# Expert work moved beside the recurrent layer, parts of the row work and of the gathers moved ahead, and one PSUM bank fewer for the decays

## The chip, the cores and the metric

The kernel runs on one core of a Trainium2 chip. That core has five engines that run side by side: PE (TensorE, matrix products), DVE (VectorE), ACT (ScalarE, functions from tables), POOL (GpSimd) and SP (SyncE, which only issues transfers here). Each engine takes its instructions in the order in which the program gave them to it. They wait for each other by semaphores. The metric is the time of one execution in microseconds (us), and the number given for a kernel is the median of its runs.

## The reference, cut to what matters

The input is x with 4 batches of 32 x 96 tokens of 256 features. Two layers follow each other.

```python
# layer 0: two Mamba blocks, along the 96 positions ("t"), then along the 32 variables ("d")
h = exp(dt * A) * h + dt * B * u          # a recurrence over the tokens, 16 states per channel
y = (h * C).sum(states) ; ...
# layer 1, attention: every pair of the 3072 tokens of a batch, 32 units
e = (tanh(q[:, :, None, :] + k[:, None, :, :] + bh) @ Wa) + ba ; t = t + softmax(e) @ t_norm
# layer 1, graph and experts, on rows that are normalized again
h = x @ W_gat ; a_src, a_dst = per-head sums
e = leaky_relu(a_src[src] + a_dst[dst])   # 1048576 random edges, softmax by destination
scores -> layer norm -> top 2 of 4 experts -> softmax gates g
out = out + g[..., ei] * (gelu(x @ W1[ei] + b1[ei]) @ W2[ei] + b2[ei])    # all 4 experts, all rows
```

The indices of the edges reach past the 12288 rows: an edge with a destination outside is dropped, one with a source outside counts for the last row, and the others are sorted into 432 columns of 128 edges and gathered. Expert work is independent of the graph until the gates weigh it.

## The kernel before, in words

The work is laid out in three stretches.

**Layer 0 (class `Layer0`)** works in 64 blocks of 384 tokens. A block has 48 slots. In two of three slots there is a pair of decays on ACT (line 371, `dA<-dt`: an exponential per state, into PSUM), the matching pair of scans on DVE (line 388, `h<-dA,dB`) and a product on POOL (line 395). The decays go round robin through `DA_BUFS` = 3 PSUM banks, so that ACT may be up to three decays ahead of the scans. The front of the next block (projections, convolution, softplus) runs in the same slots; its softplus uses two tiles, `ua` and `ub`.

**Attention (class `Attention`)** of a batch has 768 columns. In each column ACT takes a tanh over 128 x 3072 (line 790, `th<-krep,qsel`), and PE multiplies it by the weights of the units (line 766, `pe<-th`) two columns later. Every eighth column a unit ends: a maximum on DVE, an exponential on ACT (line 841, `pr`), transposes (line 848) and values (line 857) on PE. Every fourth unit ends a tile of 128 rows, for which POOL writes four small tiles (line 907, `sf`) that PE waits for. Keys of the next batch (`keys`) and the normalization of finished rows (`after`, one run of 24 tiles for a batch) are taken a step at a time from the list `side`, in columns with nothing else to do.

`whole` weaves the two: one column of attention for one slot of layer 0, written out by hand in a fixed order for PE, ACT, DVE and POOL. Layer 0 of the first batch runs alone. Attention of batches 0 to 2 then runs beside layer 0 of the later batches; these are the shared stretches. When layer 0 has ended, attention of the last batch runs beside the sorting of the edges (class `Edges`, on DVE, with one-hot products on PE) and beside `Experts.early`. `early` works on *units*: a unit is one expert on one block of 512 rows, and there are 24 blocks and 4 experts, 96 units. `early` is given budgets of PE time per column, covers the blocks of the first two batches expert by expert, and stores results in DRAM (`kept`). When attention ends, `after` of the last batch runs, four steps of `early` to each of its steps.

**The tail (`tail`)** does the units that are left and the graph. POOL gathers for each of the 432 edge columns one row of `tab_s` (by source) and one of `tab_d` (by destination), both on line 1253. 36 parts of 12 columns are scored on DVE and ACT and placed by PE (line 1294, `pa`), in four quarters; after a quarter its gates are computed, and kept results of its blocks are read back, weighed and added (line 1503). The order is a list of slots: three slots to a unit, a gather every `PART`/2 slots.

Of the kernel before, what the change touches and what calls it, by code (L numbers as in the profile page):

```python
# [26 lines left out]
P = 128  # L27
# [12 lines left out]
DA_BUFS = 3  # L40
# [4 lines left out]
KQ = TOK // NQT  # L45
LAG = 2
# [15 lines left out]
G0, PART = 4, 8  # L62
# [11 lines left out]
class Layer0:  # L74
# [8 lines left out]
    def __init__(self, ctx, tc, ident, a, x1):  # L83
# [5 lines left out]
        self.dram = pool("l0d", 1, space=bass.MemoryType.DRAM)  # L89
        ps_a = pool("l0a", 1, space=PSUM)  # L90
        self.dA = [ps_a.tile([P, 512], F32, tag=f"dA{i}", name=f"dA{i}") for i in range(DA_BUFS)]
        self.turn = 0
# [67 lines left out]
    def scale_states(self, t):  # L160
        nc = self.nc
        nc.scalar.activation(t["A"], t["A"], AF.Exp)
        nc.vector.tensor_scalar(t["A"], t["A"], -1.0, None, ALU.mult)
        nc.vector.tensor_scalar(t["D"], t["D"], 0.5, None, ALU.mult)

    def front(self, blk, lead):
# [94 lines left out]
        def _():  # L261
# [8 lines left out]
            v["ua"] = wk.tile([P, EC, T], F32, tag="ua", name="ua")  # L270
            v["ub"] = wk.tile([P, EC, T], F32, tag="ub", name="ub")
# [265 lines left out]
    def run(self):  # L537
# [34 lines left out]
        for n, blk in enumerate(blocks):  # L572
# [16 lines left out]
            for slot in range(48):  # L589
# [13 lines left out]
                if slot == 42 and then:  # L603
# [4 lines left out]
                    if fresh:  # L608
                        self.wf = self.weights(blocks[n + 2]["way"], FRONT)
                        self.scale_front(self.wf)  # L610
                yield (old["b"] if old and slot == 11 and (old["way"], old["i"]) == ("d", NBLK - 1)
# [11 lines left out]
class Attention:  # L623
# [4 lines left out]
    def __init__(self, ctx, tc, ident, a, x1, x2, xn2T, tab_s, tab_a):  # L628
# [31 lines left out]
        self.extra, self.entry = 0.0, 0  # L660
# [11 lines left out]
    def inverse_roots(self, mv):  # L672

        rs = self.rows.tile([P, NT], F32, tag="lrs", name="lrs")
        self.nc.scalar.activation(rs, mv[:, :, 1], AF.Sqrt, bias=self.eps)
        self.nc.vector.reciprocal(rs, rs)
# [21 lines left out]
    def keys(self, b):  # L698
# [13 lines left out]
        krep = self.rows.tile([P, TOK], F32, tag="krep", name="krep")  # L712
        qsel = self.rows.tile([P, TOK // R_ATT], F32, tag="qsel", name="qsel")
# [40 lines left out]
    def units(self, side):  # L754
# [24 lines left out]
        while i < B * PER + LAG or todo:  # L779
            b, col = self.entry, _ = divmod(i, PER)  # L780
# [36 lines left out]
            if b and col == LAG + 10:  # L817
                side.append(self.after(b - 1))
# [3 lines left out]
        side.append(self.after(B - 1))  # L822
# [104 lines left out]
    def after(self, b):  # L927

        nc, mv = self.nc, self.state[b]["mv2"]
        N = NT // CT  # L930
        x2 = self.x2[b * TOK:(b + 1) * TOK, :]
        x = self.tiles_of(x2, 0)
        rs = self.inverse_roots(mv)
        yield
        for j in range(N):
# [27 lines left out]
            nc.sync.dma_start(self.tab_a[:, n0:n0 + CT, :], db)  # L963
# [3 lines left out]
class Edges:  # L967
# [6 lines left out]
    def __init__(self, ctx, tc, a):  # L974
# [8 lines left out]
        self.nc.sync.dma_start(self.lanes, a["lanes"])  # L983

# [51 lines left out]
    def sort(self):  # L1036
# [4 lines left out]
        with ExitStack() as ctx:  # L1041
# [60 lines left out]
            for of, rows in ((s3, self.si), (x3, self.di)):  # L1102
# [3 lines left out]
                v.tensor_scalar(hi, d, 7, None, ALU.logical_shift_right)  # L1106
                v.tensor_tensor(flat(rows), lo, hi, ALU.add)
# [58 lines left out]
class Graph:  # L1166
# [4 lines left out]
    def __init__(self, ctx, tc, a, ed, tab_s, tab_a, tab_d, gates):  # L1171
        self.nc, self.ed = tc.nc, ed
        self.tab_s, self.tab_a, self.tab_d, self.gates = tab_s, tab_a, tab_d, gates
# [28 lines left out]
    def tables(self):  # L1202
# [3 lines left out]
        adst = new("adst", [P, NH, 2 * HEADS])  # L1206
        nc.sync.dma_start(hall, self.tab_s)
        nc.sync.dma_start(adst[:, :, 0:HEADS], self.tab_a)
# [5 lines left out]
        top, topa = new("top", [P, HEADS]), new("topa", [P, HEADS])  # L1214
        nc.vector.tensor_reduce(top, hall[:, :, 0:HEADS].rearrange("p n h -> p h n"), AX.X, ALU.max)
# [5 lines left out]
        nc.sync.dma_start(self.tab_d, adst)  # L1221
# [23 lines left out]
    def gather(self, j):  # L1245
        nc, ed = self.nc, self.ed
        gs = self.wk.tile([P, GP, ROW], F32, tag="gs", name="gs", bufs=4)
        gd = self.wk.tile([P, GP, 2 * HEADS], F32, tag="gd", name="gd", bufs=4)
        q, c0 = divmod(j * GP, CQ)
        rows = lambda t: t.rearrange("p n f -> (p n) f")  # L1250
        for u in range(GP):
            for to, table, idx in ((gs, self.tab_s, ed.si), (gd, self.tab_d, ed.di)):
                nc.gpsimd.indirect_dma_start(  # L1253
                    out=to[:, u, :], out_offset=None, in_=rows(table),
                    in_offset=bass.IndirectOffsetOnAxis(ap=idx[:, q, c0 + u:c0 + u + 1], axis=0))
        self.got[j] = gs, gd

    def scores(self, j):
        nc = self.nc
        gs, gd = self.got.pop(j)  # L1260
        e = self.wk.tile([P, GP, HEADS], F32, tag="e", name="e")
        v = self.wk.tile([P, GP, ROW], F32, tag="v", name="v")
# [602 lines left out]
```

## Time and profile before

| what | value |
|---|---|
| median of 3 runs | 15634.05 us (15623.67 to 15639.06) |
| profiled execution | 15643.13 us, its span 15641.4 us |
| busy, share of the span | PE 75%, DVE 71%, ACT 77%, POOL 58% |
| layer 0 of the first batch, alone | 0 to about 2560 us |
| shared stretches with the changes of batch | about 2560 to 11150 us |
| attention of the last batch, edges, early units | to 13988 us |
| rows of the last batch, early units | to 14198 us |
| tail | 14198 to 15641 us |

Times inside the profile are counted from the span's start. A row of the groups gives line, engine, operation, the tiles written and read, their shapes and a count; behind the first bar the busy time and the mean of one in ns; behind the second the idle time of the engine just before them and what ended it. PE records an fp32 product twice. A row of the stages gives the length, then for PE, weight loads, DVE, ACT and POOL busy time and count, then the granted clock of PE, the share of the DMA engines and GB/s.

### The profile page before, as it was taken

The numbers are of one execution on the slowest core, as the hardware profiler recorded it, in microseconds if no ns is written. First come the engines' busy times: TensorE is split into PE (matmuls) and PEld (weight loads), VectorE is DVE, ScalarE is ACT, GpSimd is POOL, SyncE is SP. The second block draws the span as 40 slices with busy tenths as digits, with TensorE's granted clock in tenths as the row PEclk, the third lists the DMA queues.
The fourth block names the chain that finished last, engine by engine and source line by source line (L and its number), as shares of the span: only waits on it lengthen the run. The fifth ranks groups of instructions, "written<-read, shape, count | busy, mean of one in ns | idle before, by whom it ended". The sixth has DMA issues, their size and how long they took to land.

```text
span 15641.4 us, 222408 instructions
## 1 busy us (share of the span) xinstructions
PE 11808.2 (75%) x85872; PEld 5087.3 (33%) x85872; DVE 11045.8 (71%) x15303; ACT 12053.9 (77%) x9331; POOL 9052.0 (58%) x6586
## 2 busy tenths in 40 slices
PE   5666665777777767777777777777778788889988
PEld 2222222222222232222223322222233344446545
DVE  7888888777777787777778876777677733323455
ACT  3443335999999979999998899999979899971211
POOL 4555557777777767777777675777500000004774
PEclk8888886888888888888888888888889999999999
DMA  5666665444445444444444443454310000013223
GB/s 188 203 202 203 199 198 160 149 145 151 148 146 150 154 151 145 145 148 147 148 149 150 151 147 115 143 152 151 121 47 28 17 8 8 21 36 82 43 62 101
DMA packets 1168144, 1959.71 MB, mean 125 GB/s; under 512 B 408545, under 2 KB 612961, under 8 KB 1164897
## 3 DMA queue, kind: packets, MB, share of 16 engines
q1 hardware_dynamic: 1139424, 1939.16, 39.8%
q0 software_dynamic: 27648, 6.25, 0.8%
q8 instruction: 675, 11.06, 0.3%
q14 instruction: 397, 3.24, 0.1%
HBM read 1841.73 MB, written 103.28 MB: 124 GB/s over the span
## 4 chain that ended last, share of the span: by engine, by line
ACT 37%; PE 20%; DVE 17%; POOL 12%; issue 10%; DMA 4%; SPq 0%; DVEq 0%; POOLq 0%; ACTq 0%
ACT th L790 27%; PE pe L766 9%; DVE h L388 6%; ACT dA L371 6%; POOL h L395 4%; POOL gs L1253 3%; POOL gd L1253 3%; PE pv L857 2%; DVE dB L379 2%; ACT pr L841 2%; DMA bB<-bc 2%; PE ptw L848 1%; PE po L1432 1%; POOL ub L305 1%; PE ph L1424 1%
## 5 line engine op out<-in xcount | busy, mean ns | idle before, releaser
L790 ACT ACTIVATE th<-krep,qsel 128x3072 f32<-128x3072 f32 x3072 | 8666.3, 2848 | 327.1 <-PE pe L766 309.7
L766 PE MATMUL pe<-th,wa_blk 128*32 128x384 f32 x49152 | 5118.1, 547 | 1893.1 <-ACT pr L841 1536.3
L395 POOL TENSOR_TENSOR h<-h,bC 128x768 f32<-128x768 f32 x2048 | 3785.0, 1848 | 2561.5 <-DVE h L388 2310.8
L388 DVE TENSOR_TENSOR_SCAN h<-dA,dB 128x384 f32<-128x384 f32 x4096 | 3683.3, 940 | 787.4 <-ACT dA L371 601.8
L766 PEld LDWEIGHTS pe<-th,wa_blk 128*32 128x32 f32 x49152 | 1472.2, 118 | 4581.0 <-issue 1989.1
L379 DVE TENSOR_TENSOR dB<-bB,dtu 128x768 f32<-128x768 f32 x2048 | 1946.2, 950 | 131.7 <-DMA bB<-bc 87.5
L371 ACT ACTIVATE dA<-dt,t_A 128x380 f32<-128x380 f32 x2048 | 1122.1, 570 | 879.6 <-DVE h L388 873.9
L907 POOL TENSOR_SCALAR sf<-sel,f 128x32 f32<-128x32 f32 x384 | 152.5, 421 | 2639.2 <-ACT f L903 2522.0
L371 ACT ACTIVATE dA<-dt,d_A 128x372 f32<-128x372 f32 x2048 | 1097.8, 562 | 557.3 <-DVE h L388 551.8
L414 PE MATMUL py<-h,ident 128*128 128x384 f32 x2176 | 1000.6, 592 | 680.0 <-POOL h L395 678.7
L402 POOL TENSOR_TENSOR h<-h 128x768 f32<-128x768 f32 x752 | 1422.9, 1892 | 46.6
L850 DVE COPY pT<-ptw 128x512 f32<-128x512 f32 (+1 forms) x768 | 425.7, 554 | 1149.6 <-PE ptw L848 1148.4
L857 PE MATMUL pv<-xn,pT 128*32 128x257 f32 x18432 | 1090.6, 384 | 84.3 <-DVE pT L850 83.5
L414 PEld LDWEIGHTS py<-h,ident 128*128 128x128 f32 x2176 | 438.1, 219 | 1243.8 <-POOL h L395 1016.1
L403 POOL TENSOR_TENSOR h<-h 128x384 f32<-128x384 f32 x752 | 803.0, 1068 | 59.0
L404 POOL TENSOR_TENSOR y<-y,h 128x384 f32<-128x384 f32 x752 | 773.7, 1029 | 59.0
L857 PEld LDWEIGHTS pv<-xn,pT 128*32 128x32 f32 x18432 | 584.4, 111 | 638.3 <-DVE pT L850 169.5
L1500 ACT ACTIVATE h<-ph,b 128x512 f32<-128x512 f32 x248 | 165.2, 686 | 702.8 <-PE ph L1424 702.4
L1253 POOL DMA_INDIRECT gs<-tab_s,si x432 | 501.6, 1161 | 131.7 <-issue 127.1
L1253 POOL DMA_INDIRECT gd<-tab_d,di x432 | 487.3, 1128 | 134.7 <-issue 130.1
L309 DVE SCALAR_TENSOR_TENSOR ua<-ub,ua 128x384 f32<-128x384 f32 x256 | 429.2, 1677 | 190.5 <-POOL ub L305 186.3
L1432 PE MATMUL po<-w,h 128*128 128x256 f32 x1984 | 471.9, 393 | 54.7 <-DVE o L1493 38.4
(280 smaller groups left out, 14868.4 us busy)
## 6 DMA issues: line engine op xcount, KB each, us to landing
bB<-bc SPq DMA_DIRECT2D x2048, 384.0 KB
bC<-bc SPq DMA_DIRECT2D x2048, 384.0 KB
x<-x SPq DMA_DIRECT2D x144, 256.0 KB
kept<-ko SPq DMA_DIRECT2D x68, 512.0 KB
all<-kept SPq DMA_DIRECT2D x17, 2048.0 KB
xt<-xn2T SPq DMA_DIRECT2D x59, 512.0 KB
x<-x SPq DMA_DIRECT2D x192, 128.0 KB
xs<-in_xT SPq DMA_DIRECT2D x16, 768.0 KB
```

The costliest lines, as they stand in the source:

```text
L371: nc.scalar.activation(inner(dA[:, :T]), inner(blk["dt"][:, e, :]), AF.Exp, scale=blk["w"]["A"][:, e, i + s:i + s + 1])
L379: nc.vector.tensor_tensor(dB, blk["bB"].pop(j), z["dtu"].unsqueeze(1).to_broadcast([P, SB, T]), ALU.mult)
L388: nc.vector.tensor_tensor_scan(h[:, s, :], z.pop(("dA", e, i + s))[:, :T], z["dB"][:, s, :], 0.0, ALU.mult, ALU.add)
L395: nc.gpsimd.tensor_tensor(h, h, blk["bC"].pop(j), ALU.mult)
L402: nc.gpsimd.tensor_tensor(h0, h0, h1, ALU.add)
L403: nc.gpsimd.tensor_tensor(h0[:, 0, :], h0[:, 0, :], h0[:, 1, :], ALU.add)
L404: nc.gpsimd.tensor_tensor(y[e], y[e], h0[:, 0, :], ALU.add)
L414: nc.tensor.matmul(z["py"], self.ident, h[:, s, :], start=(i == 0), stop=(i == DS - 1))
L766: nc.tensor.matmul(pe[q * QU:(q + 1) * QU, j, :KQ // 2], self.wa[:, k, :], th[:, c0:c0 + KQ // 2], start=(k == 0), stop=(k == NK - 1))
L790: nc.scalar.activation(th, s["krep"], AF.Tanh, bias=s["qsel"][:, col:col + 1])
L857: nc.tensor.matmul(pv[q * QU:(q + 1) * QU, :C + 1], pT[:, i, q * QU:(q + 1) * QU], s["xn"][:, q * NK + i, :], start=(i == 0), stop=(i == N ...
L1253: nc.gpsimd.indirect_dma_start(out=to[:, u, :], out_offset=None, in_=rows(table), in_offset=bass.IndirectOffsetOnAxis(ap=idx[:, q, c0 + u: ...
```

## The change

It has several parts.

- **`Beside`**: 25 jobs in the slots of the shared stretches. A job is three half units (256 rows each) of one expert. In a block's 48 slots it has six pairs of products (slots 0 to 12), one gelu over 128 x 3072 on ACT (slot 14), and six output products (slots 15 to 29). Each product goes into one new PSUM bank, which DVE drains a slot later. Weights, rows and bias lie in the tiles that the keys of the next batch will take.
- `DA_BUFS` falls from 3 to 2: its bank is the one that `Beside` uses. `ua` and `ub` become one tile, `uab`, which takes turns with the hidden units of a job (`eh`).
- `after` of a batch runs in four parts, as its tiles end, each with its own inverse roots.
- Of 432 gathers by destination, 324 (first three batches) are issued in attention of the last batch, three to a column, once the edges are sorted; they read `tab_a`, now a table for each batch. `tab_d` goes; what it held is computed for each part on DVE. The gathers of a part are put ten slots ahead of its scores, and the first ahead of the tables.
- `early` covers three batches, without the units that `Beside` has done.

Counted in the two programs' instruction lists, units fall as follows: beside layer 0, from 0 to 37 (and a half); in `early`, from 34 to 22; in the tail, from 62 to 37.

```diff
-DA_BUFS = 3
+DA_BUFS = 2
+AFTER = (0, 8), (8, 16), (16, 22), (22, 24)
...
-G0, PART = 4, 8
+G0, PART = 10, 6
...
-            v["ua"] = wk.tile([P, EC, T], F32, tag="ua", name="ua")
-            v["ub"] = wk.tile([P, EC, T], F32, tag="ub", name="ub")
+            uab = self.wide("uab")
+            for i, k in enumerate(("ua", "ub")):
+                v[k] = uab[:, i * EC * T:(i + 1) * EC * T].rearrange("p (e t) -> p e t", e=EC)
...
+                if self.beside:
+                    self.beside(slot, then is None or then["way"] != blk["way"] == "d")
                 yield (old["b"] if old and slot == 11 and (old["way"], old["i"]) == ("d", NBLK - 1)
...
-        krep = self.rows.tile([P, TOK], F32, tag="krep", name="krep")
-        qsel = self.rows.tile([P, TOK // R_ATT], F32, tag="qsel", name="qsel")
+        krep, qsel = self.krep[b % 2], self.qsel[b % 2]
...
             if b and col == LAG + 10:
-                side.append(self.after(b - 1))
+                side.append(self.after(b - 1, *AFTER[-1]))
+            side += [self.after(b, t0, t1) for t0, t1 in AFTER[:-1]
+                     if b < B and col == t1 * P // R_ATT + LAG + 10]
...
+    def gather(self, q, c):
+        if (q, c) not in self.have:
+            self.have.add((q, c))
+            self.nc.gpsimd.indirect_dma_start(
+                out=self.gd[:, q, c, :], out_offset=None,
+                in_=self.tab_a[q].rearrange("p n f -> (p n) f"),
+                in_offset=bass.IndirectOffsetOnAxis(ap=self.di[:, q, c:c + 1], axis=0))
...
-        nc.sync.dma_start(self.tab_d, adst)
...
-            for to, table, idx in ((gs, self.tab_s, ed.si), (gd, self.tab_d, ed.di)):
-                nc.gpsimd.indirect_dma_start(
...
+            nc.gpsimd.indirect_dma_start(
+                out=gs[:, u, :], out_offset=None, in_=rows,
+                in_offset=bass.IndirectOffsetOnAxis(ap=ed.si[:, q, c0 + u:c0 + u + 1], axis=0))
+            ed.gather(q, c0 + u)
...
-        nc.vector.tensor_tensor(e, e, gd[:, :, HEADS:], ALU.subtract)
+        nc.vector.tensor_tensor(sh, gd, self.topa.unsqueeze(1).to_broadcast([P, GP, HEADS]), ALU.add)
+        self.leaky(sh)
+        nc.vector.tensor_tensor(e, e, sh, ALU.subtract)
...
+class Beside:
+    PRODUCTS = {0: (0, 0), 3: (0, 1), 5: (1, 0), 8: (1, 1), 10: (2, 0), 12: (2, 1)}
+    GELU = 14
+    OUTPUTS = {15: (0, 0), 17: (0, 1), 20: (1, 0), 23: (1, 1), 26: (2, 0), 29: (2, 1)}
...
+        if (not self.jobs or last or att.asked > att.entry + 1 or att.col < 40
+                or self.jobs[0][0] >= min(att.normed, att.entry)):
+            return
+        b, e, j = self.job = self.jobs.pop(0)
+        place = att.krep[(att.entry + 1) % 2]
...
+            if slot - 1 in self.PRODUCTS:
+                k, f2 = self.PRODUCTS[slot - 1]
+                for f in (2 * f2, 2 * f2 + 1):
+                    nc.vector.tensor_scalar(self.h[:, k, f, :], self.ps[:, f % 2, :],
+                                            self.b1[:, e, f:f + 1], None, ALU.add)
+            if slot - 1 in self.OUTPUTS:
...
+                nc.vector.tensor_tensor(o, self.ps[:, 0, :], self.b2, ALU.add)
+                i, n = divmod(self.first + k, 2)
+                nc.sync.dma_start(self.kept_block(i)[:, 2 * n + q, e, :], o)
+            if slot in self.PRODUCTS:
+                k, f2 = self.PRODUCTS[slot]
+                self.ps = self.bank()
+                for f in (2 * f2, 2 * f2 + 1):
+                    for c in range(KC):
+                        nc.tensor.matmul(self.ps[:, f % 2, :], self.w1[:, c, f * P:(f + 1) * P],
+                                         self.xt[:, c, :], start=(c == 0), stop=(c == KC - 1))
...
+            if slot == self.GELU:
+                h = self.h.rearrange("p k f m -> p (k f m)")
+                nc.scalar.activation(h, h, AF.Gelu)
...
-            t = 3 * G0 + PART * m // 2
-            at(t, lambda j=j: gr.gather(j))
-            t += 10
+            t = G0 + PART * m // 2
+            if m < 1:
+                gr.gather(j)
+            else:
+                at(max(0, t - 10), lambda j=j: gr.gather(j))
             at(t, lambda j=j: gr.scores(j))
...
-                    if units is None and att.entry == B - 1:
+                    if units is None and att.entry == B - 1 == att.normed:
...
-                            [(i, e) for e in range(NEXP) for i in range(NBLK_X // 2)], a, place)
+                            [(i, e) for i in range(NBLK_X - NBLK_X // B) for e in range(NEXP)
+                             if (i, e) not in ex.done], a, att.krep[B % 2])
...
+                    for _ in range(3 if columns else 0):
+                        ed.gather(*columns.pop(0))
```

## The prediction

> **What bounds the kernel now.** I read first the page's slices, then the stages, then the groups of the bounding engine, then the order of time where two stages meet. The slices of ACT and POOL:
>
> ```profile
> ACT  3443335999999979999998899999979899971211
> POOL 4555557777777767777777675777500000004774
> ```
>
> ACT is full from slice 7 to slice 35, but for the two changes of batch; POOL is idle for eight slices and busy again at the end. The stages (length; then PE, weight loads, DVE, ACT, POOL) say it in numbers:
>
> ```profile
> 2560.00:5400.00 2840.00, 2107.10 (x18009) 787.81 (x18008) 2212.24 (x2860) 2754.95 (x2079) 2205.30 (x1573) 0.86 0.48 149
> 6000.00:8300.00 2300.00, 1708.61 (x14680) 627.48 (x14676) 1783.25 (x2248) 2233.65 (x1686) 1792.68 (x1279) 0.87 0.47 147
> 12500.00:13990.00 1490.00, 1307.73 (x13684) 602.23 (x13688) 473.75 (x877) 1445.44 (x588) 20.41 (x60) 0.94 0.04 13
> 14230.00:15485.00 1255.00, 1133.12 (x3414) 671.13 (x3413) 580.36 (x963) 254.71 (x336) 987.44 (x863) 0.95 0.28 65
> ```
>
> In both shared stretches and in the attention of the last batch ACT is busy 97%: what is added to ACT there lengthens the kernel, what is added to PE, DVE and POOL may fit. In the tail POOL has 987 us of 1255, and between its gathers 0.30 us of issue each:
>
> ```profile
> L790 ACT ACTIVATE th<-krep,qsel 128x3072 f32<-128x3072 f32 x3072 | 8666.3, 2848 | 327.1 <-PE pe L766 309.7 <-DVE krep L733 11.4
> L1253 POOL DMA_INDIRECT gs<-tab_s,si x432 | 501.6, 1161 | 131.7 <-issue 127.1 <-DMA gs<-tab_s,si 4.6
> L1253 POOL DMA_INDIRECT gd<-tab_d,di x432 | 487.3, 1128 | 134.7 <-issue 130.1 <-DMA tab_d<-adst 3.3 <-DMA gs<-tab_s,si 1.2
> ```
>
> So a gather costs 1.145 + 0.30 = 1.45 us there, 864 of them 1253 us, which is the stage. The tail is POOL's until 15485; PE needs less, since one unit, 16 records of `ph` and twice 16 of `po`, takes 13.77 us once gathers are over (15543.11 to 15556.88):
>
> ```profile
> 15543.11 3.62 PE L1432 MATMUL po<-w,h 128*128 128x256 f32 x16
> 15546.56 1.88 PE L1424 MATMUL ph<-xt,w 128*128 128x512 f32 x4
> 15548.28 3.62 PE L1432 MATMUL po<-w,h 128*128 128x256 f32 x16
> 15551.73 5.31 PE L1424 MATMUL ph<-xt,w 128*128 128x512 f32 x12
> 15556.88 3.62 PE L1432 MATMUL po<-w,h 128*128 128x256 f32 x16
> ```
>
> 62 units at 13.77 and 108 placings at 3.38 us make 1219 us.
>
> **Gain: from the end of attention (13988) to the end.** Before this takes 15641 - 13988 = 1653 us: 242 until gathers start at 14230 (12 units of `early` and twelve pairs of tiles of `after` lie there), 36 parts x 34.8 = 1253, then 158. After, by the instruction lists: one pair of tiles and one pair of units are left, and the first part's gathers stand ahead of the tables. POOL needs the last write of `tab_s`: the pair of tiles takes about 36 us (before, its first ran from 14001 to 14027, and here its rows must first be written and read back). Parts 0 to 8 still gather both tables: 9 x 24 x 1.45 = 313. The other 27 gather 12 x 1.45 = 17.4 us each, less than PE's share of a part, one unit and three placings: 13.77 + 10.14 = 23.9. PE sets these: 27 x 23.9 = 645, and 6% for waits on `rh`, 39 (PE was busy 86 to 90% there while it waited for POOL; I take a third of that). PE trails POOL by 13. The last gates take 22 (15516 to 15541 before, with other work between). Then six blocks of kept results: 16 additions x 0.485 = 7.8 us, about 10 with their reads, 60, and 10 for the last store. Sum 36 + 313 + 13 + 645 + 39 + 22 + 70 = 1138. **Gain 515**; 440 if additions wait for their 2 MB reads, 560 if POOL's quieter price (0.94 + 0.30) holds.
>
> **Cost 1: ACT in the shared stretches.** 25 gelus of 3072 are new. No such row exists; the nearest are gelu of 2048 (1.91 us) and tanh of 3072 (2.848), so 2.85 x 25 = 71. Each needs other tables than the exponentials. The lists show 235 table loads ahead of the tail after against 164 before: 50 by gelus, 24 by 12 more inverse roots, three fewer elsewhere. What one costs:
>
> ```profile
> 13886.55 1.28 ACT L1467 ACT_TABLE_LOAD   x1
> 13887.85 3.71 ACT L1467 ACTIVATE h<-h 128x2048 f32<-128x2048 f32 x2
> ```
>
> 1.30 from its start to the next start, and it begins 0.02 after the tanh ends. The Trainium skill, "ScalarE: Activation LUTs", "What ACT_TABLE_LOAD costs", adds a drain of 1.38 us to a switch, 2.66 in all. By the rule 71 loads cost 189 us, by the row 92. I see no drain in this row (before the load the tanh has its usual 2.84) and take 92. With 3 for the roots **166 us**, all on the bound; 263 by the rule.
>
> **Cost 2: two banks for decays.** With three, decay k waits for scan k-3; with two, for scan k-2. I set the recorded start of every decay in the trace against the recorded end of scan k-2. In layer 0 alone decays come later, but no scan would: ACT is under 40% busy there and finishes a decay while DVE is at the next scan and product. In the shared stretches, if everything else stayed put, new waits sum to 114 us (69, 38 and 7); if a delay once taken is never made up but moves all, 12. Most of the 114 would fall into gaps ACT has anyway. **40**, and 10 at the changes of batch (16 and 148 by the same ways; ACT is not the bound there).
>
> **Cost 3: PE and DVE of the jobs.** A product of 512 rows and half the columns costs PE 0.45 us (16 records 3.62), so a slot with a piece gets 1.8 us more. A column lasts about 3.6 us (one tanh and four thirds of a decay) and holds 2.66 of PE (74%): 4.5 in 12 of 32 slots, 2.66 in the rest. ACT may run two columns ahead of PE (three `th` tiles, two columns' lag), which covers 0.9 us and the 0.9 of the next piece; where a piece meets a unit's values (2.8 us) it doesn't. About one such meeting a job at 1.2 us: **30**, between 0 and 120. Draining costs DVE 7.6 us a job (18 x 0.42), under its 78% load; if that cover were gone it would be 190. Each job adds to SP three row loads behind PE's products, six stores behind DVE, and at times weights; the reads of `bB` and `bC` stand behind them, two ahead of need. I take nothing, for SP's waits are on work of the same slot.
>
> **Cost 4: gathers ahead.** The list puts all 324 gathers into attention's last four tiles, 96, 96, 96 and 36 between the `sf` groups. POOL takes them in order, ahead of `sf`:
>
> ```profile
> 13712.56 1.36 POOL L907 TENSOR_SCALAR sf<-sel,f 128x32 f32<-128x32 f32 x4 [92.58 <-ACT f L903]
> 13814.26 1.36 POOL L907 TENSOR_SCALAR sf<-sel,f 128x32 f32<-128x32 f32 x4 [100.35 <-ACT f L903]
> 13917.55 1.36 POOL L907 TENSOR_SCALAR sf<-sel,f 128x32 f32<-128x32 f32 x4 [101.93 <-ACT f L903]
> ```
>
> 96 gathers at 1.25 are 120 us, and a tile lasts 94 to 103. So `sf` comes 28, 20 and 18 us late; PE's product of the tile waits in order behind it, then the scores, then ACT: 66 less two columns of slack, **60**. The price per gather is where a second rule speaks: "SBUF — State Buffer", "SBUF: two separate sides", the "DVE blocks DMA" trap, says that DVE instructions lock POOL out while it writes descriptors. In the tail the rows agree that it can be dear (0.94 at best, up to 2.92). At 1.45 the cost would be 120. I take 1.25 since DVE is 18% busy there against 46% in the tail, and mostly reads PSUM.
>
> **Cost 5, the rest.** `after` of the last batch moves from behind attention into it: 12 steps of 2.4 us on PE at 88% load, half of it lost, 15. Layer 0 ends at column 2238, not 2243, so five columns of 3.1 us follow it: 15. `early` does 20 units before attention ends in both lists. The merged `uab` has the same waits as two tiles had: nothing; it is free of `eh` four slots before it is written.
>
> **Sum.** 166 + 50 + 30 + 60 + 30 = 336; 515 - 336 = 179. Against the profiled span 15641 - 179 = 15462, an execution of 15464; the median lies 9 below the profiled execution, so **15455 us**.
>
> **Rivals.**
> - *ACT's gaps take the jobs* (0.2): ACT idles 2.5% of 8100 us, about 190, mostly for PE. A pass of 5.4 us on ACT lets PE and DVE catch up, so costs 1 to 3 shrink to about 130 and the gain's upper end holds: 15310. For: idle of `th` behind PE is 310. Against: the stages at 97%.
> - *The tail stays dear* (0.2): gather and additions hinder each other, with gain 420, and `sf` late by 100: 15590. For: gathers of 2.9 us. Against: DVE gets no more work there.
> - *PE becomes the bound beside jobs* (0.1, slower): if two columns of slack are used up already (in the first stretch PE waited 365 us behind `pr`, up to 13 us at once, and has that to catch up), each of 300 pieces costs ACT 0.9 us: 270 in place of 30, and lateness of the drains delays gelu. 15455 + 240 + 20 = 15715. It decides from 0.66 us a piece. Against: PE is idle a quarter of the time.
> - *It doesn't do what it says*: the list shows 25 gelus and 37 tail units, so no.
>
> **How the numbers follow.** My own case has 0.5, with 15340 to 15600. Range over all: 15285 to 15650; below lies half of the first rival, above most of the third. A difference of 0.2%, 31 us, is what a measurement of this kernel tells from none. Faster 0.85 (own case 0.48, first rival 0.2, second 0.17), same 0.05, slower 0.10.
>
> **What would show it.** Right: a tail of about 1140 us from the last tanh, with PE over 90% busy in its second half; 25 gelus of 2.85 us each between two loads; `sf` late in three tiles; no new DVE wait for decays in layer 0 alone. Wrong: ACT idle behind PE in columns with pieces, over 150 us more than before; or parts of the tail that still follow at 30 us or more.

## Result and profile after

The changed kernel takes 15479.64 us (median of 4 runs, 15476.97 to 15495.72) against 15636.56 before, measured beside it: a ratio of 0.9901, 95% interval 0.9884 to 0.9918. The prediction was 15455. The profiled execution has a span of 15478.4 us, 163 less than before; the prediction's sum was 179. A second comparison on another chip, told below, gave 1.0018, and there the kernel before is slower as well (15811.90 us): what the change is worth depends on something that the trace of before did not show.

The slices of ACT and POOL in the page of the changed kernel (40 slices of 387 us):

```profile
ACT  3443334999999979999999899999998989998221
POOL 4565557777777767777777677577750000007663
```

POOL is idle for six slices, where it was for seven before, and slice 37 has 7 tenths of POOL in place of 4: gathers now run while attention ends. ACT stays full to slice 37 of 40, one more than before. Next the stages of the changed kernel: the second shared stretch with jobs, the third, the last attention ahead of the gathers, the same with gathers, and the later tail (length; then PE, weight loads, DVE, ACT, POOL busy; clock, DMA share, GB/s):

```profile
5950.00:8400.00 2450.00, 1999.08 (x15973) 868.97 (x15973) 1839.78 (x2523) 2314.73 (x1722) 1777.09 (x1267) 0.90 0.49 149
9150.00:11450.00 2300.00, 1889.51 (x15422) 810.88 (x15421) 1660.41 (x2313) 2205.88 (x1612) 1615.36 (x1161) 0.90 0.48 145
12800.00:13890.00 1090.00, 966.60 (x10368) 459.83 (x10364) 404.61 (x778) 1055.98 (x430) 14.96 (x44) 0.93 0.04 12
13890.00:14352.00 462.00, 348.71 (x3266) 153.05 (x3262) 80.25 (x160) 388.06 (x163) 313.47 (x340) 0.88 0.17 29
14740.00:15400.00 660.00, 621.40 (x1838) 355.28 (x1836) 474.98 (x875) 149.44 (x187) 354.92 (x302) 0.96 0.33 83
```

PE rose from 74% to 82% in the shared stretches, and ACT is still busy 94 to 96%. While gathers run, ACT has 388 of 462 us (84%); the run without them, below, shows what that cost. In the tail PE has 94% and POOL 54%, where POOL had 79% before: the bound has moved to PE, as the prediction said. The groups of the changed kernel that answer to those of before:

```profile
L802 ACT ACTIVATE th<-krep,qsel 128x3072 f32<-128x3072 f32 x3072 | 8665.9, 2847 | 406.0 <-PE pe L778 389.2
L1286 POOL DMA_INDIRECT gs<-tab_s,si x432 | 504.7, 1168 | 265.2 <-issue 121.8
L1009 POOL DMA_INDIRECT gd<-tab_a,di x432 | 428.3, 991 | 133.0 <-issue 133.0
```

The tanh waits 79 us more in all. The gather by destination is 0.14 us cheaper on the average: the three quarters of them that run in attention, where DVE is mostly idle, have a median of 0.95 us. The other gather costs what it did (1168 against 1161). The trace of before fits: of the 864 gathers in its tail 192 took more than 1.1 us, and DVE was at work during 92% of their time, against 29% of the others'. In order of time, PE in the tail, four `sf`, and ACT around the gelu of a job:

```profile
14806.40 3.38 PE L1333 MATMUL pa<-rh,ol 128*128 128x480 f32 x8
14809.62 1.88 PE L1577 MATMUL ph<-xt,w 128*128 128x512 f32 x4
14811.34 3.62 PE L1585 MATMUL po<-w,h 128*128 128x256 f32 x16
14814.79 3.38 PE L1333 MATMUL pa<-rh,ol 128*128 128x480 f32 x8
```

```profile
13817.34 1.36 POOL L921 TENSOR_SCALAR sf<-sel,f 128x32 f32<-128x32 f32 x4 [94.11 <-ACT f L917]
13912.87 1.36 POOL L921 TENSOR_SCALAR sf<-sel,f 128x32 f32<-128x32 f32 x4 [94.17 <-ACT f L917]
14034.31 1.37 POOL L921 TENSOR_SCALAR sf<-sel,f 128x32 f32<-128x32 f32 x4
14156.20 1.36 POOL L921 TENSOR_SCALAR sf<-sel,f 128x32 f32<-128x32 f32 x4
```

```profile
9333.83 2.85 ACT L802 ACTIVATE th<-krep,qsel 128x3072 f32<-128x3072 f32 x1
9336.70 1.28 ACT L1497 ACT_TABLE_LOAD   x1
9337.99 2.76 ACT L1497 ACTIVATE eh<-eh 128x3072 f32<-128x3072 f32 x1
9340.66 2.84 ACT L802 ACTIVATE th<-krep,qsel 128x3072 f32<-128x3072 f32 x1
9343.52 1.28 ACT L378 ACT_TABLE_LOAD   x1
```

PE goes from one product to the next without a gap. The third and fourth `sf` have no idle time before them: POOL came late from 96 gathers, 121.4 and 121.9 us apart. And a job is one gelu and two loads, 5.3 us, with a tanh between them that needs neither load.

Cut at the starts of tanh columns (0 is the first of attention; 3071 the last), the two profiled executions compare so:

| stretch | before | after | difference |
|---|---|---|---|
| start to column 0 | 2581.7 | 2568.3 | -13.4 |
| columns 0 to 2240, shared with layer 0 | 8713.3 | 9031.3 | +318.0 |
| columns 2240 to 2816 | 1911.1 | 1898.9 | -12.2 |
| columns 2816 to 3071, gathers in the changed kernel | 778.9 | 851.0 | +72.1 |
| last tanh to the end | 1656.5 | 1128.9 | -527.6 |

So attention ends 365 us later (336 predicted) and what follows is 528 shorter (515 predicted). Both terms are near; the runs below show which parts of the 336 were right. The start of column 0 is not stable: it varies by 17 us between profiles of the same code (see the runs without jobs).

My first reading of these two traces was another one. Between columns 0 and 2240 ACT's waits of decays for scans rose from 173 to 303 us, its waits of tanh for PE only from 158 to 170. That looked as if two banks had cost 130 us (predicted: 50) and PE's share of the jobs nothing (predicted: 30). The experiments were laid out to tell this theory from the prediction's own.

### The profile page after: what moved, and what is told of

It is laid out like the page before. It is cut to its first block, busy times and chain, and to the rows that moved or that the text cites. A ratio compares the mean times of both kernels' runs of the same rounds, so it can differ in the third digit from the quotient of the medians.

```text
span 15478.4 us, 224265 instructions
## 1 busy us (share of the span) xinstructions
PE 11840.1 (76%) x86496; PEld 5192.8 (34%) x86496; DVE 11076.9 (72%) x15711; ACT 12181.5 (79%) x9326; POOL 8984.7 (58%) x6586
## 4 chain that ended last, share of the span: by engine, by line
ACT 32%; PE 23%; DVE 19%; POOL 11%; issue 10%; DMA 4%; SPq 0%; DVEq 0%; POOLq 0%; ACTq 0%
ACT th L802 23%; PE pe L778 9%; DVE h L395 7%; POOL h L402 5%; ACT dA L378 5%; POOL gd L1009 3%; PE pv L871 2%; DVE dB L386 2%; DMA bB<-bc 2%; PE pa L1333 2%; PE po L1585 1%; ACT pr L855 1%; PE ph L1577 1%; PE ptw L862 1%; POOL uab L312 1%
## 5 line engine op out<-in xcount | busy, mean ns | idle before, releaser
L1286 POOL DMA_INDIRECT gs<-tab_s,si x432 | 504.7, 1168 | 265.2 <-issue 121.8
L316 DVE SCALAR_TENSOR_TENSOR uab<-uab 128x384 f32<-128x384 f32 x256 | 389.8, 1523 | 198.6 <-POOL uab L312 194.6
L1659 ACT ACTIVATE h<-ph,b 128x512 f32<-128x512 f32 x148 | 100.4, 687 | 533.3 <-PE ph L1577 533.1
L1009 POOL DMA_INDIRECT gd<-tab_a,di x432 | 428.3, 991 | 133.0 <-issue 133.0
L848 DVE TENSOR_REDUCE nb<-pe 128x1 f32<-128x768 f32 x384 | 362.1, 943 | 197.2 <-PE pe L778 197.0
```

The costliest lines, as they stand in the source:

```text
L1009: self.nc.gpsimd.indirect_dma_start(out=self.gd[:, q, c, :], out_offset=None, in_=self.tab_a[q].rearrange("p n f -> (p n) f"), in_offset=b ...
```

## Experiments

The first four kernels ran on one chip, which behaves as in the profile of the result. The other eight ran in two sets, each on a further chip. There before takes 15827.36 and 15811.90 us, 1.2 to 1.3% more than on the first; no profile of before was taken there. What the profiles of the changed kernel show of the difference is told with the runs on gathers, and columns 0 to 2240 don't contain it. The changed kernel's code for these columns was profiled six times, on both kinds of chip, and took 9023.8 to 9034.5 us, a spread of 11 us. So kernels are compared in these columns across sets, and by medians only within a set.

### Two banks alone

```diff
 # kernel before
-DA_BUFS = 3
+DA_BUFS = 2
```

> The kernel before with one change, two PSUM banks for the decays. The theory as predicted: +50 us against before, 40 in the shared stretches by ACT waiting for scans, 10 at the changes of batch, nothing in layer 0 alone. The theory formed from the two traces (two banks are the dear part, the jobs are not): ACT's waits of decays for scans rise by about 100 to 130 us between columns 0 and 2240, as they did in the changed kernel, layer 0 alone is about 13 us shorter as it was there, sum +85 to +115. The rival (the longer waits come from the jobs' own draining work on DVE, which delays the scans): +30 or less.

Measured: 15678.14 us against 15623.00, ratio 1.0034 (1.0022 to 1.0047): +55 us, where the prediction said 50. In the columns 0 to 2240 it is 8763.6 against 8713.3, +50.3. ACT's waits in these columns, of before and then of this kernel (engine, line, what was waited for; us in all, times, longest):

```profile
ACT dA L371 <- DVE h L388: 173.3, 118, 7.9
ACT th L790 <- PE pe L766: 157.6, 173, 6.5
ACT pr L841 <- DVE nb L834: 58.4, 49, 4.2
```

```profile
ACT dA L371 <- DVE h L388: 261.9, 315, 7.9
ACT th L790 <- PE pe L766: 131.8, 148, 6.8
ACT pr L841 <- DVE nb L834: 30.1, 33, 4.2
```

The waits for scans grew by 89 us, but 54 us of other waits went: the waits of tanh for PE and of exponentials for DVE are shorter, as they would be if PE and DVE catch up while ACT stands at a decay. ACT's idle time grew by only 33 us (401 to 434). The other 18 of the 50 are busy time (8312.2 to 8329.8 us) for the same instructions, of unchanged lengths: two that follow each other on ACT overlap by some 0.09 us, and one that had to wait doesn't. A wait's growth is not its cost. My reading of the two traces had made that mistake; the theory built on it (+85 to +115) falls. The changes of batch, for which 10 us were put down, took no longer (columns 736 to 783: 273.4 against 273.7; 1504 to 1551: 230.8 against 234.9).

### No jobs, with two banks and with three

```diff
 # changed kernel, class Beside
-        self.jobs = [(b, e, j) for b in range(B - 2) for e in range(NEXP) for j in range(n)]
+        self.jobs = []
```

> The changed kernel with no jobs beside layer 0 (their units are done in the early work and in the tail), still two banks. Read from column 0 to column 2240 against the changed kernel: 166 by predicted cost 1 plus 30 by cost 3 = 196 us shorter if the jobs cost what was predicted; about 136 to 166 shorter if PE's and DVE's part of the jobs costs nothing and ACT's part is 5.45 us a job plus the inverse roots, which stay here; over 250 shorter if the jobs' draining work on DVE is what makes decays wait. The tail is longer by 38 units of about 14 us or by less where gathers fill, so the whole is slower than the changed kernel by 200 to 350 us.

```diff
 # the kernel without jobs
-DA_BUFS = 2
+DA_BUFS = 3
```

> The kernel without jobs, with three banks in place of two. The difference to the kernel without jobs and with two banks, columns 0 to 2240, is what two banks cost with no job beside them: 40 us by the prediction, 100 to 130 by the theory that two banks are the dear part, under 30 by the rival that only the jobs' work on DVE makes the waits. Layer 0 alone: 13 us longer than with two banks.

Measured: 15677.18 us with two banks and 15616.49 with three, on the same chip: 61 us. In the columns 0 to 2240: 8813.0 and 8761.0, 52 us, 6 of them at the two changes of batch. That is the cost of two banks a second time, with all other parts of the change in place, and again the prediction's size. Against the changed kernel the jobs cost 218 us in these columns (9031.3 - 8813.0), where 196 had been expected with the inverse roots counted in and 136 to 166 by my reading after the result. What remains without jobs and with three banks, 8761.0 against 8713.3, is 48 us. I put it down to the rows' normalization in four parts; no run has that part of the change alone (`uab` and the doubled keys are in it too). ACT's busy time there grew by 26 of them (8312 to 8339), with table loads ahead of tanh (62.9 to 71.8 us) and of the roots (5.1 to 16.7 us); 30 had been predicted. The other 21 are idle time, whose cause stays open.

The first tanh starts at 2553.1 and 2553.8 in these two: layer 0 alone doesn't care for the third bank, as predicted. The 13 us by which the changed kernel reached it sooner, which I had taken for an effect of two banks, are no such thing: kernels with the same code up to there start it anywhere from 2551.6 to 2568.3. The whole kernel without jobs was expected 200 to 350 us slower than the changed one. Each set against its own before, it is 211 slower (54 above, 157 below): its tail grew by 413 us, not by 38 x 13.8.

### The pass on ACT, its table loads, and what is left

```diff
 # changed kernel, class Beside
-                nc.scalar.activation(h, h, AF.Gelu)
+                nc.scalar.activation(h, h, AF.Tanh)
```

> The changed kernel with tanh in place of gelu in the hidden units of the jobs (25 passes over 3072 elements): the length of the pass is about the same (2.85 us), the two table loads around each are gone, 50 in all. By the row of the trace before (1.30 us a load, on the engine that sets the time): 65 us shorter. By the rule of a drain (2.66 us a load): 133 shorter. By the rival that gaps of ACT take the jobs: under 20 shorter. This part of the computation is changed: the jobs' units come out with another function.

```diff
 # changed kernel, class Beside
             if slot == self.GELU:
-                h = self.h.rearrange("p k f m -> p (k f m)")
-                nc.scalar.activation(h, h, AF.Gelu)
+                pass
```

> The changed kernel with the jobs' pass on ACT left out, so that the jobs are only products on PE, drains on DVE and transfers; the hidden units of the jobs stay without a function. By predicted cost 1: 71 + 65 = 136 us shorter than the changed kernel. By the rival that gaps take the jobs: under 60 shorter. What is left against the kernel without jobs, columns 0 to 2240, is cost 3, PE and DVE of the jobs: 30 us by the prediction, 270 by the rival that PE becomes the bound beside jobs, about 0 by the reading of the two traces.

Measured, columns 0 to 2240: 9031.3 with gelu, 8962.9 with tanh, 8903.2 without the pass, 8813.0 without jobs. (The whole kernels took 15786.63 and 15731.10 us on a chip of the second kind, where before took 15827.36; these medians are not set against those of the first chip.) So:

- 50 table loads cost 68.4 us, 1.37 each; 65 had been predicted from the 1.30 of the row, 133 by the drain of 1.38 us that the Trainium skill adds to a load ("ScalarE: Activation LUTs", "What ACT_TABLE_LOAD costs"). No drain is seen here: ACT's idle time is 530 us in both kernels, and its busy time grew by the 68. The passes have the same length (2.76 and 2.75 us). The 0.07 over the row fit the overlap of 0.09 that a load takes away: in the rows above, the tanh at 9340.66 starts before the gelu ends at 9340.75, while the load at 9336.70 starts after the tanh has ended.
- 25 passes cost 59.7 us, 2.4 each, where a pass lasts 2.76. All of ACT's part together: 128, predicted 136. The rival in which ACT's gaps take the jobs (under 60) falls: this work lengthens the stretch almost one for one. With a spread of 11 us between profiles of one code, each of these differences is good to about 10 us.
- PE's products and DVE's drains of the jobs, with nothing on ACT, cost 90.2 us, three times the 30 that the prediction took, and within its 0 to 120. By the reading of the two traces it was to be 0.

ACT's waits in these columns without the jobs, and then with the jobs but without their pass, show where the 90 are:

```profile
ACT dA L378 <- DVE h L395: 287.6, 357, 7.4
ACT th L802 <- PE pe L778: 111.9, 127, 4.8
```

```profile
ACT dA L378 <- DVE h L395: 297.4, 355, 7.4
ACT th L802 <- PE pe L778: 184.1, 189, 5.5
```

Tanh waits 72 us more for PE, and decays 10 more for scans. Column by column, these sums mislead again. All of the lengthening lies in the 840 columns from the first piece of a job to three behind its last (3096.7 to 3184.7 us; the 664 others from column 736 on took 2863.7 and 2865.8, though tanh waits 23 us more in them). ACT in the 840 columns:

| ACT, us (waits) | without jobs | jobs without their pass |
|---|---|---|
| tanh waits for PE, in the seventh column of each eight | 16.7 (14) | 47.1 (38) |
| tanh waits for PE, in the other seven | 24.8 (27) | 43.6 (54) |
| decays wait for scans | 19.8 (51) | 40.0 (56) |
| busy | 3032.1 | 3040.0 |

The seventh column is the one behind a unit's values (they run while the fifth and sixth tanh are the latest begun). There 30 us come in, 24 waits for 25 jobs: the one meeting a job at 1.2 us that the prediction put down, and the seven profiles of kernels whose jobs have a pass and two banks are at 48 to 55 us there. The third rival's toll on every piece is not seen: the other seven columns have 19 us more, 0.06 a piece, where it put 0.9. What the prediction did not have is the rest: these 19, 20 of decays, 8 of overlap lost, and some 11 in pauses that this view doesn't resolve. DVE's drains of the jobs stand ahead of scans, which would make decays wait; no run has the drains alone.

The parts add to the whole: 48 (rows in four parts) + 52 (banks) + 68 (loads) + 60 (passes) + 90 (PE and DVE) = 318. Each is the difference of two profiles, in a row from before to the changed kernel, so that the sum comes out by construction; what is tested is each size against its prediction.

### Gathers ahead, and a second kind of chip

```diff
 # changed kernel
-                            columns = [(q, c) for q in range(B - 1) for c in range(CQ)]
+                            columns = []
```

> The changed kernel with none of the 324 gathers by destination issued in the attention of the last batch; all are done in the tail. By predicted cost 4 the attention of the last batch is 60 us shorter (columns 2816 to 3071: 851 to about 785), and the 27 parts of the tail that took 24.7 us take 34.8 as the first nine do, 270 us longer: +210 us. By the rival that gathers ahead cost little because the late sf are taken up by slack: attention shorter by under 20 us, +250. By the dearer price (1.45 us a gather): attention shorter by 120, +150.

Measured, in the set of the first chip: 15694.40 us against 15623.00 of before, ratio 1.0045 (1.0029 to 1.0061). Each set against its own before, that is 228 above the changed kernel (71 above, 157 below). Columns 2816 to 3071 take 783.6 us against 851.0: the gathers ahead cost 67, predicted 60. ACT's waits in these columns, without the gathers and with them, show the predicted way, tanh behind PE, and all of the 67:

```profile
ACT th L802 <- PE pe L778: 16.4, 31, 1.3
```

```profile
ACT th L802 <- PE pe L778: 83.4, 45, 24.2
```

The tail takes 1416 us against 1129, its later parts 35.5 us each against 24.7. Without the gathers ahead the whole change is slower than before, so they carry its gain.

```diff
 # changed kernel: two gathers to a column, the others left for all parts alike
-                            columns = [(q, c) for q in range(B - 1) for c in range(CQ)]
+                            columns = sorted(((q, c) for q in range(B - 1) for c in range(CQ)),
+                                             key=lambda qc: qc[1] % GP >= 9)
...
-                    for _ in range(3 if columns else 0):
+                    for _ in range(2 if columns else 0):
```

> The changed kernel with 2 gathers to a column of the last attention instead of 3, and the ones that stay behind shared out over all parts of the first three batches (three in each, where POOL has time beside PE). By predicted cost 4 the 60 us of late sf go, since 64 gathers to a tile take 80 to 93 us and a tile lasts 94 or more; the tail's parts stay at about 25 us since POOL then has 15 gathers x 1.45 = 21.8 us a part: 60 to 70 us shorter in sum. If the tail's parts become POOL's at 15 to 16 gathers a part: +2 us a part, 27 parts, so 5 to 15 shorter only.

Measured: 15779.06 us, with before at 15827.36 in the same set, ratio 0.9973 (0.9958 to 0.9989). The columns with gathers took 1087.8 us, not the 785 to 790 that the expectation implies, and `sf` came 174 us apart. The same stood in the other three profiles of that set (1179 to 1183 us, with 96 gathers to a tile), and it needed the changed kernel beside them to tell what the change is worth there. In a further set, on a third chip:

> The changed kernel once more, so that it stands on the same chip as the three beside it. On a chip such as the one of the first comparison: 0.990 of before, last attention 2816 to 3071 in about 851 us. On a chip such as the one of the runs with tanh, without the pass, with gathers spread and with the bank lent (there PE and ACT stood still while 96 gathers ran, and the same columns took 1180 us): 15855 us against 15827 of before, 1.002, by 15787 + 68 and 15731 + 128.

Measured: **15842.27 us against 15811.90 of before, ratio 1.0018 (1.0010 to 1.0026)**. Here the change makes the kernel no faster (30 us slower). The columns to 2240 take 9023.8 us, as on the first chip; columns 2816 to 3071 take 1178.9 against 851.0, and the rest 1173.7 against 1128.9. The stages of the last attention on this chip: without gathers, a run of gathers, then the rest of that tile.

```profile
13600.00:13785.00 185.00, 157.48 (x1717) 77.67 (x1719) 61.29 (x113) 181.66 (x75) 2.72 (x8) 0.94 0.03 8
13905.00:14010.00 105.00, 21.15 (x49) 4.76 (x49) 0.42 (x1) 5.71 (x2) 77.47 (x83) 0.50 0.09 5
14010.00:14105.00 95.00, 75.28 (x653) 30.66 (x653) 13.39 (x24) 80.68 (x35) 0.00 (x0) 0.87 0.05 15
```

And one run of gathers in the profile of the result:

```profile
13913.00:14033.00 120.00, 88.45 (x838) 38.04 (x834) 19.32 (x35) 106.88 (x45) 91.17 (x99) 0.89 0.26 59
```

POOL issues its gathers at the same pace in both (0.94 to 0.95 us and 0.30 of issue). But on this one the other engines nearly stand still meanwhile: two instructions of ACT in 105 us, 49 of PE. PE's instructions, in order of time, have no semaphore before them:

```profile
13950.78 0.59 PE L871 MATMUL pv<-xn,pT 128*32 128x257 f32 x1 [2.21 <-issue]
13953.58 0.59 PE L871 MATMUL pv<-xn,pT 128*32 128x257 f32 x1 [2.21 <-issue]
13956.38 0.59 PE L871 MATMUL pv<-xn,pT 128*32 128x257 f32 x1 [2.21 <-issue]
```

One comes every 2.80 us, where 48 of them otherwise take 2.80 together. The DMA queues from 13930 to 14000, first on this chip, then in the profile of the result (queue: packets, MB, share of 16 engines):

```profile
q0 software_dynamic: 1777, 0.12, 7.7%
q14 instruction: 1, 0.01, 0.0%
```

```profile
q1 hardware_dynamic: 1042, 1.55, 7.4%
q0 software_dynamic: 1818, 0.12, 6.4%
q8 instruction: 4, 0.07, 0.4%
q14 instruction: 1, 0.01, 0.0%
```

The gathers' packets are alike. On this chip nothing else moves but one packet of q14. That SyncE's transfers (q1) are missing says little, for SP issued none between 13906 and 14027. That no packet of the kind "instruction" came on q8 would fit engines that have run out of instructions, but the end of the stretch speaks against it. The last gather ends at 14007.5; then PE comes back, and from 14007 to 14027 the gathers' last packets are all that the queues have:

```profile
14016.59 0.80 PE L778 MATMUL pe<-th,wa_blk 128*32 128x384 f32 x1 [1.31 <-issue]
14017.98 1.55 PE L778 MATMUL pe<-th,wa_blk 128*32 128x384 f32 x2 [0.59 <-issue]
14020.08 6.71 PE L778 MATMUL pe<-th,wa_blk 128*32 128x384 f32 x42 [0.55 <-issue]
```

```profile
q0 software_dynamic: 61, 0.00, 1.6%
```

PE issues 42 products in 6.7 us before the next packet of q8 (14027.9), so as far as these queues show it had its instructions, and issued them at 2.80 us each all the same. What holds the engines back stays open, and so does why: each set had its own chip and its own time, so the chip itself is not told from anything else that held during a set. The lower clock (0.50) is PE's alone and doesn't account for ACT, which does 2 instructions there in place of some 40.

The two sister kernels of this set:

> The changed kernel with 2 gathers to a column instead of 3 and the rest shared out over the tail's parts, on the same chip as the changed kernel. Where engines don't stand still during gathers: 60 to 70 us shorter than the changed kernel by cost 4, 5 to 15 if the parts of the tail get longer. Where they do: 70 to 80 shorter, 15779 against 15855.

> The changed kernel with no gathers in attention, on the same chip as the changed kernel. Where engines don't stand still during gathers: 214 us longer than the changed kernel, as once measured. Where they do: attention of the last batch is about 395 us shorter and the tail 280 longer, so about 110 shorter than the changed kernel, if gathers in the tail cost no more there than elsewhere; longer if they do.

Measured: 15760.52 us with the gathers spread and 15769.65 without gathers ahead, 82 and 73 below the changed kernel; 70 to 80 and 110 had been expected. Spreading 68 gathers over the tail's parts gave 89 us back in attention (1090.1 against 1178.9), and the parts did not get longer (mean of the later ones 24.95 against 24.84). Without gathers ahead attention's columns fall to 787.2, as on the first chip (783.6). But its tail takes 1521 us here against 1416 there, since with 24 gathers to a part PE stands still there too: from 15080 to 15220 it has 43 us of 140, where POOL issues 95 gathers. So on this kind of chip moving the 324 gathers ahead costs attention 392 us (1178.9 against 787.2) and gives the tail 348 back (1521.4 against 1173.7), where the first chip had 67 and 287. The 68 shared out over the parts cost the tail nothing (1172.1 against 1173.7).

### The third bank lent

```diff
 # changed kernel, three banks; a job's products take the third
+                    k = next(k for k in self.order if k < 2 or not self.lent)
+                    self.order.remove(k)
+                    self.order.append(k)
+                    dA = self.dA[k]
...
+                self.l0.lent = False
+                nc.vector.memset(self.l0.dA[2][:, :T].rearrange("p (q l) -> p q l", l=self.l0.L)[:, :, 0:1], 0.0)
...
+        if slot == 42 and self.job:
+            self.l0.lent = True
```

> The changed kernel, with the third bank back: the decays use three banks, and the third is lent to a job from slot 42 ahead of its block to slot 31 in it, when DVE sets its first columns to zero again. 25 of about 48 shared blocks have a job, so about half of what two banks cost comes back. With 61 us as that cost (measured without jobs): 25 to 30 us shorter than the changed kernel, and layer 0 of the first batch about 10 us longer, so 15 to 20 in sum. With 130 as that cost with jobs: half of it at most, 65 shorter. By the rival that the waits come from jobs' work on DVE: no gain, or longer by the added memsets.

> Both at once: gathers spread and third bank lent. The two act in stretches that don't touch, so the gains add: 50 us in columns 0 to 2240 by the bank (as measured with the bank alone, 8982 against 9031) and 60 to 75 by the gathers: 110 to 125 shorter than the changed kernel on either kind of chip. If the parts of the tail get longer by 15 or 16 gathers each: 55 to 65 shorter.

Measured: with the bank lent alone, columns 0 to 2240 take 8981.6 us, 46 less than the six profiles' mean; with both edits 9004.3, 23 less, by the same code in these columns. 20 us of it are in the columns to 736, where no job runs (2831 both times, 2852 to 2855 in the six); beside jobs it gave 26 once and 3 once. The expectation was 25 to 30, which lies between the two; why they differ by 23 is open. The whole kernel was at 0.9987 of before (0.9980 to 0.9995) on a chip of the second kind. Both edits together: 15748.60 us, ratio to before 0.9949 (0.9932 to 0.9965), 94 less than the changed kernel beside it (15842.27), where 110 to 125 had been expected, and the lowest median of the four on that chip; it is 12 below the gathers spread alone, but their executions overlap (15706.90 to 15758.34 and 15749.08 to 15810.68). On a chip of the first kind it was not run; the 67 us of late `sf` that spreading is meant to save there, and the 23 to 46 of the bank, stay an expectation.

## Why the prediction was right, point by point

- **Gain, 515; measured 528.** The tail from the last tanh takes 1129 us, 1138 in the sum. The first gather of the tail starts 36 us after attention ends, as put down. 27 later parts at 24.7 us: predicted 23.9 + 6% = 25.3. The first parts came at about 35 us, as by 24 gathers at 1.45. The rival of a dear tail is out here.
- **Cost 1, 166; measured 128 for the jobs and about 26 for the roots and loads of the rows' four parts, 154.** The row of 1.30 us a load was the right price but for 0.07 of lost overlap, and the rule of a drain was not. This work is on the bound: no gap took it.
- **Cost 2, 50; measured 50, 52 and 61 (the last over the whole kernel).** The reasoning that most of 114 us of new waits falls into gaps held: 89 us of new waits cost 50, of which 33 are idle time and 18 lost overlap, which the step did not have. The 10 at changes of batch were not there in the first pair (6 in the pair without jobs).
- **Cost 3, 30; measured 90.** This is the term that was mis-sized. Its step for PE, one meeting of a piece with a unit's values for each job at 1.2 us, came as put down: 30 us in the column behind the values. It put everything else at nothing: DVE's drains because DVE is under 78% busy, and PE's other columns because of two columns of slack. The runs show 20 us of decays waiting for scans, 19 of tanh in the other columns, and some 20 in lost overlap and short pauses.
- **Cost 4, 60; measured 67** (851.0 with gathers ahead, 783.6 without), at 1.25 us a gather as taken, and the way was the predicted one: `sf` late in three tiles, tanh behind PE. (The trap that the step names, in "SBUF — State Buffer" of the Trainium skill, is for DVE instructions in a two-port mode, not for all of them; no run here tells the modes apart.) But the step looked only at POOL's order and at `sf`. That gathers can hold up the other engines was in no case of the prediction, and on two chips it is the largest effect of all: 328 us more in the same columns. There before is 175 us slower as well, and the gain of 157 us becomes a loss of 30. The forecast was right for the kind of chip that its trace came from; that the result was measured on this kind too is luck.
- **Cost 5, 30; measured -12 and +5.** Columns 2240 to 2816 were shorter, not 15 longer, and the last rows cost 5 (783.6 against 778.9).

So 365 in place of 336 on one side and 528 in place of 515 on the other: PE's share of the jobs was 60 too small and the rows in parts cost 18 more, which errors the other way (8 for the jobs on ACT, 37 in cost 5) and a start 13 us earlier partly made up. That the sum came within 25 us of the median rests on this: no reasoning of the prediction made these errors cancel. Two readings of it were off without bearing on the sum: POOL is idle for seven slices before, not eight, and the terms of the first rival make 15294, not 15310.

## What to carry to other kernels

Growth of one kind of wait is not its cost: two banks added 89 us of waits and 50 us of time, since 54 us of other waits went; undo the one edit before blaming it, and look where a wait stands: 23 us of tanh's new waits lay in columns that took no longer. Work put beside a saturated engine costs its own time on that engine almost in full, and the small products beside it with their drains cost 0.3 us each (90 us for 300) even where PE is idle a quarter of the time. And measure a change that packs many small gathers together on more than one chip.

## Hardware behaviour that was not expected

On two chips of those used, a run of gathers by index (one of 128 rows every 1.25 us) nearly stopped PE, ACT and DVE for as long as it lasted: PE issued one product per 2.80 us without a semaphore to wait for, and in 70 us no packet but the gathers' own and one of q14 moved. In the profile of the result a run at the same pace left ACT busy 107 us of 120. The gathers' own rows are the same in both, so nothing in POOL's lines shows it; it is seen in PE's "issue".

Two instructions of ACT that follow each other overlap by some 0.09 us, and a wait or a table load between them takes this away: 155 more waits cost 18 us of ACT's busy time in the kernel with two banks alone.
